# Layer 1's first neighbour stage as seven half-size products in place of eight

## The chip, the cores and the metric

The kernel runs on one core of a Trainium2 chip. The metric is the device time of one execution in microseconds (us); a shorter time is better. Before the change the median of three runs is 2171.74 us (2170.61 to 2173.77). The core has a matrix engine (TensorE, PE in the profile, with its weight loads as PEld), three engines for elementwise work (VectorE or DVE, ScalarE or ACT, GpSimd or POOL), and a queue engine for loads (SyncE or SP). Matrix products are written to PSUM, everything else lies in SBUF.

## The reference, cut to what matters

The program is a network of two layers on a graph of 625 nodes with 1024 features each. Layer 0 (edge attention, linear attention, a small quantised feed-forward) and most of layer 1 (linear attention, attention, a mixture of eight experts) are not touched. What is touched is the graph part of layer 1:

```python
def _sage_layer(h, edge_src, edge_dst, deg_inv, W_self, W_neigh, b):
    msg = h[edge_src]
    agg = jax.ops.segment_sum(msg, edge_dst, num_segments=h.shape[0])
    mean = agg * deg_inv[:, None]
    return h @ W_self + mean @ W_neigh + b
h = jax.nn.relu(_sage_layer(x, edge_src, edge_dst, deg_inv, W_self0, W_neigh0, b0))
out = _sage_layer(h, edge_src, edge_dst, deg_inv, W_self1, W_neigh1, b1)
```

Here `x` is the normalised input. The first of the two layers, with its relu, is "the first neighbour stage": a product of the pair (x, mean), 625 x 2048, with the stacked weights (W_self0 above W_neigh0), 2048 x 1024. All of it is fp32. The residual `x + out + attention` also gets two bias rows, `b1` of this part and `bo` of the attention.

## The kernel before, in words

Features lie on the partitions: `xnT1`, `meanT` and `hT` hold 1024 features as 8 blocks (`KC`) of 128 partitions, with 626 columns, one for each node and one of padding, taken as two halves of 313 (`HN`). A matmul takes a 128x128 block of weights and 313 columns. `feat` (it calls `group`, L137, whose line all these matmuls carry) makes one block of 128 output features: for each half of the columns a sum over 16 pairs, 8 of them with `xnT1` and 8 with `meanT`. The first neighbour stage calls it for the 8 output blocks `m`; ScalarE adds the bias `b0_t` and applies the relu in one instruction (L1274). Weights come as `Half` tiles: two loads of 1 MB for 512 of the 1024 output columns, from the pool `wpool` with six buffers of 1 MB.

The order of the instructions on the engines around the change is written out by hand: what stands first in the program stands first in its engine's queue. `do(prep, pe, after, after2)` is a small pipeline: each call first runs the pending `after` steps of earlier calls, then issues its own matmuls, and keeps its own `after` for the next call. PSUM tiles of two banks (`ps2`) exist three times, so the fourth user waits for what reads the first.

Four stages follow each other here. First comes the linear attention's query loop: for each `m`, `lin1.query(m + 1)` (16 matmuls into `pq`, then two ScalarE activations and L340 on VectorE for `qf`) and `lin1.answer(m)` (two matmuls into `pd`, two into `po`; then on VectorE L356 on `pd`, a reciprocal L357, and L358, which multiplies `po` into `oT`). In the first five rounds `rows_of(1, m)` is called as well: L1215 normalises 512 columns of x, and ScalarE and L1196 split the result into a high and a low part (`xnh`, `xnl`). Second comes the mean stage, `pa`: for each `k`, 20 matmuls with the adjacency counts `CTr`, and then two multiplications by the inverse degree on VectorE (L1253), which write `meanT`. The last `answer` lies inside it, at `k == 1`. Third comes the first neighbour stage, `ph`. Fourth comes `neighbours(0)`, with 40 matmuls into `pz` that read `hT`, and then `last_of`, which reads x (`px`).

At `m == 0` and `m == 4` of the first neighbour stage SP also loads a bias row (`b1`, then `L1_bo`) into `b_t`, and GpSimd adds it to the five tiles of x (L1266, ten instructions). GpSimd's queue reaches them as soon as the row has landed, whatever TensorE is at. Behind them stand two small loads for `g_t`, and stores of zeros to `rows_d` and `y_d`, whose source tile `zero` is set by L1313.

Of the kernel before, what the change touches and what calls it, by code (L numbers as in the profile page):

```python
# [8 lines left out]
FP = mybir.dt.float32  # L9
# [4 lines left out]
AF = mybir.ActivationFunctionType  # L14
ALU = mybir.AluOpType
# [5 lines left out]
NT = 5  # L21
P = 125
NP = 626
HN = 313
# [5 lines left out]
D = 1024  # L30
KC = D // 128
# [11 lines left out]
def gps_kernel(tc: tile.TileContext, w: dict, out: bass.AP):  # L43

    again = attempt(tc, w, out, False)
    with tc.If(again > 0):
        attempt(tc, w, out, True)  # L50
# [3 lines left out]
def attempt(ctx: ExitStack, tc: tile.TileContext, w: dict, out: bass.AP, shifted: bool):  # L54

    nc = tc.nc
# [10 lines left out]
    def ps2(name):  # L67
        return psums[-1][0].tile([128, 2, 512], FP, tag="ps2", name=name, bufs=3)
# [44 lines left out]
    class Half:  # L113


        def __init__(self, pool, src, c, tag="w", padded=None, now=True):
            v = src.rearrange("(k p) n -> p k n", p=128)
            self.parts = []

            def load():  # L120
                i = len(self.parts)
                t = pool.tile([128, 4, 512], FP, tag=tag, name="w", padded_shape=padded)
                self.parts.append(t)
                return nc.sync.dma_start(out=t, in_=v[:, 4 * i:4 * i + 4, c * 512:(c + 1) * 512])

            self.load = lambda: behind(load(), latest["pe"])
            if now:
                load()
                load()
# [4 lines left out]
    def group(dst, pairs):  # L134

        for i, (lhsT, rhs) in enumerate(pairs):
            made = nc.tensor.matmul(dst, lhsT=lhsT, rhs=rhs, start=(i == 0), stop=(i == len(pairs) - 1))  # L137
        latest["pe"] = made.ins.name
# [3 lines left out]
    def behind(ins, name):  # L142

        tc.add_manual_dep(ins.ins, name, mybir.DependencyInfo(mybir.DependencyClass.Sync,
                                                              mybir.DependencyReason.DATA), reason="pace")
        return ins

    def feat(name, pairs):

        p = ps2(name)  # L150
        for h in range(2):
            group(p[:, h, :HN], [(a, b[:, h * HN:(h + 1) * HN]) for a, b in pairs])
        return p[:, :, :HN]

    def halves(ap):
        return ap.rearrange("p (h n) -> p h n", h=2)
# [32 lines left out]
    class Stream:  # L189
# [7 lines left out]
        def __call__(self, prep=None, pe=None, after=None, after2=None):  # L197
            if prep is not None:
                prep()
            for steps in self.open:  # L200
                if steps:
                    steps.pop(0)()
            self.open = [steps for steps in self.open if steps]
            if pe is not None:
                pe()
            self.open.append([f for f in (after, after2) if f is not None])
# [15 lines left out]
    do = Stream()  # L222
    hold = {}

    def mid(shape, name):
        return midp.tile(shape, FP, tag="mid", name=name)

    def bigT(name):
        return big.tile([128, KC, NP], FP, tag="big", name=name, padded_shape=[128, KC, 640])
# [133 lines left out]
    with ExitStack() as st0:  # L363
# [8 lines left out]
        with ExitStack() as edges:  # L372
# [22 lines left out]
            def load_edges():  # L395
                for dst, name in ((si, "src"), (di, "dst")):
# [16 lines left out]
                                      in_=none.unsqueeze(1).to_broadcast([128, 28, 440]))  # L413
# [398 lines left out]
            for m in range(KC):  # L812
# [11 lines left out]
                if m < 3:  # L824
# [3 lines left out]
                                             in_=w[("w_gate", "w_up", "w_down")[m]]  # L828
# [9 lines left out]
            kept = mid([P, 2, 512], "kept")  # L838
# [18 lines left out]
        x = xpool.tile([P, NT, D], FP, name="x")  # L857
# [245 lines left out]
        for p in range(NT + 2):  # L1103
# [15 lines left out]
            if p == 0:  # L1119
                xnT1 = bigT("xnT1")  # L1120
# [40 lines left out]
    few = ctx.enter_context(tc.tile_pool(name="few", bufs=1, side="right", reuse_waits="tile"))  # L1161
# [1 line left out]
    sage = mixed_up.enter_context(tc.tile_pool(name="sage", bufs=1, reuse_waits="tile"))  # L1163
    dinv = sage.tile([128, NP], FP, name="dinv")
    dinvT = few.tile([P, NT], FP, name="dinvT")
    b0_t = mix.tile([128, KC], FP, tag="bq", name="b0_t", bufs=2)
    nc.gpsimd.dma_start(out=b0_t, in_=w["b0"])

    def degrees():
# [40 lines left out]
    def rows_of(c, t):  # L1210
        if c:
            xh = mix.tile([P, 512], FP, tag=("kb", "ke")[t % 2], name="xh", bufs=1)
        else:
            xh = mix.tile([128, NP], FP, tag="qf", name="xh", bufs=2)[:P, 0:512]
        nc.vector.tensor_scalar(xh, x[:, t, c * 512:(c + 1) * 512], mv1[:, t, 0:1],  # L1215
                                rs1[:, t:t + 1], op0=ALU.subtract, op1=ALU.mult)
        split(xh, xnh[c][0][:, t, :], xnh[c][1][:, t, :])
# [12 lines left out]
    for m in range(KC - 1):  # L1230
        lin1.query(m + 1)
        lin1.answer(m, oT)
        if m < NT:
            rows_of(1, m)
    meanT = []
    for k in range(KC):
        if k == 1:
            lin1.answer(KC - 1, oT)
        if k % 4 == 0:
            meanT.append(mid([128, 4, NP], "meanT"))  # L1240

        def pe():
            p = hold["pa"] = ps2("pa")

            for h in range(2):
                group(p[:, h, 0:HN + 1], [(xp[:, s, k % 4 * 128:k % 4 * 128 + 128],
                                           CTr[:, s, h * (HN - 1):h * (HN - 1) + HN + 1])
                                          for xp in xnh[k // 4][:1 if shifted else 2] for s in range(NT)])

        def after(k=k):  # L1250
            m = meanT[k // 4][:, k % 4, :]
            for h in range(2):
                nc.vector.tensor_tensor(m[:, h * HN:(h + 1) * HN], hold["pa"][:, h, h:h + HN],  # L1253
                                        dinv[:, h * HN:(h + 1) * HN], op=ALU.mult)

        do(None, pe, after)
    hT = []
    for m in range(KC):
        if m % 4 == 0:
            ws, wn = Half(wpool, w["W_self0"], m // 4), Half(wpool, w["W_neigh0"], m // 4)  # L1260
            hT.append(mid([128, 4, NP], "hT"))

            b_t = mix.tile([128, D], FP, tag="kv", name="b_t", bufs=2)
            nc.sync.dma_start(out=b_t, in_=w[("b1", "L1_bo")[m // 4]].to_broadcast([128, D]))
            for t in range(NT):
                nc.gpsimd.tensor_tensor(x[:, t, :], x[:, t, :], b_t[:P], op=ALU.add)  # L1266
        a = m % 4

        def pe():
            hold["ph"] = feat("ph", [(ws(k, a * 128, 128), xnT1[:, k, :]) for k in range(KC)]  # L1270
                              + [(wn(k, a * 128, 128), meanT[k // 4][:, k % 4, :]) for k in range(KC)])

        def after(m=m):
            nc.scalar.activation(halves(hT[m // 4][:, m % 4, :]), hold["ph"], AF.Relu, bias=b0_t[:, m:m + 1])  # L1274

        do(None, pe, after)
    z, ws, wo = [], [], []

    def neighbours(c):

        zc = big.tile([P, 2, NT, 512], NUM, tag="big", name="z")
        z.append(zc)
        wn1 = Half(wpool, w["W_neigh1"], c)
        ws.append(Half(wpool, w["W_self1"], c))
        wo.append(Half(wpool, w["L1_Wo"], c))
        for t in range(NT):
            def pe():
                hold["pz"] = ps1("pz")
                group(hold["pz"][:P], [(hT[k // 4][:, k % 4, nodes(t)], wn1(k)) for k in range(KC)])

            def after(t=t):
                split(hold["pz"][:P], zc[:, 0, t, :], zc[:, 1, t, :])

            do(None, pe, after)

    neighbours(0)
    mixed_up.close()


    rows_d = dram.tile([N + 1, D], FP, name="rows_d")  # L1300
# [15 lines left out]
    for b in range(NB_MIN, NB):  # L1316
        nc.gpsimd.dma_start(out=y_d[b * 128:(b + 1) * 128, :].rearrange("p (a n) -> p a n", a=4),
                            in_=zero.unsqueeze(1).to_broadcast([128, 4, 256]))
# [61 lines left out]
    wq = [Half(wpool, w["Wq"], c) for c in range(2)]  # L1380
# [247 lines left out]
    hT = bigT("hT")  # L1628
# [82 lines left out]
    def small(name):  # L1711
        return pool.tile([P, NT], FP, name=name)
# [10 lines left out]
    for i in range(2):  # L1723
        m = small(f"best{i}")
# [4 lines left out]
        first = small(f"first{i}")  # L1729
# [6 lines left out]
    e2, p1 = small("e2"), small("p1")  # L1736
# [7 lines left out]
    both = pool.tile([P, NT, NE], FP, name="both")  # L1744
# [146 lines left out]
    with tc.manual_schedule(engines={mybir.EngineType.PE, mybir.EngineType.DVE, mybir.EngineType.Pool}):  # L1891
        def fetch(t):

            pair = []
            for i, (tag, n) in enumerate((("xg", 2), ("yb", 2))):
                yg = pool.tile([128, D], FP, tag=tag, name="yg", bufs=n)
                nc.gpsimd.indirect_dma_start(out=yg, out_offset=None, in_=y_d[:, :],
                                             in_offset=bass.IndirectOffsetOnAxis(ap=place[:, i, t:t + 1], axis=0))
                pair.append(yg)
            return pair  # L1900
# [14 lines left out]
        pairs = [fetch(0), fetch(1)]  # L1915
# [97 lines left out]
```

## Time and profile before

| what | value |
|---|---|
| median of three runs | 2171.74 us (2170.61 to 2173.77) |
| the profiled execution, its time | 2175.02 us |
| its span, first to last instruction | 2173.3 us |
| mean granted TensorE clock | 0.987 |
| TensorE, VectorE, ScalarE, GpSimd busy | 96%, 33%, 9%, 15% of the span |
| query loop and last query, first `pq` to first `pa` | 666.05 to 757.08 us |
| mean stage, first `pa` to first `ph` | 757.08 to 786.80 us |
| first neighbour stage, first `ph` to first `pz` | 786.80 to 921.66 us |
| `pz`, first to first `px` | 921.66 to 955.99 us |
| GpSimd's additions to x (L1266) | five at 725.02 to 737.60, five at 858.01 to 869.58 us |
| memory traffic | 301.63 MB, mean 139 GB/s |

All times of stages are microseconds from the start of the span of the one profiled execution, which is 3.3 us above the median. An fp32 matmul of the program is two records of the profile. The duration of a matmul record is that of a pipelined instruction; what it costs is read from the distance between starts. Busy time of an engine says nothing of waits: the waits stand in brackets in the timeline.

### The profile page before, as it was taken

How to read it: one execution, taken by the hardware profiler on the slowest of the kernel's cores; microseconds unless marked ns; L12 is line 12 of the kernel's file. 1: busy time of each engine (PE TensorE's matmuls, PEld its weight loads, DVE VectorE, ACT ScalarE, POOL GpSimd, SP SyncE). 2: the span in 40 equal slices, each digit the busy share in tenths (PEclk: the TensorE clock that was granted, in tenths of full speed). 3: DMA queues.
4: the chain of work that ended last, by engine and by line, in shares of the span. 5: the costliest groups of instructions: out<-in, count | busy, mean ns of one | idle time of the engine just before them, and what ended most of it. 6: DMA issues, size and time to landing. Idle time of an engine off the chain costs nothing. (4 is left out here: it accounts for less than half of the span.)

```text
span 2173.3 us, 17398 instructions
## 1 busy us (share of the span) xinstructions
PE 2096.6 (96%) x6934; PEld 1202.3 (55%) x6934; DVE 712.4 (33%) x1214; ACT 194.4 (9%) x355; POOL 327.6 (15%) x329
## 2 busy tenths in 40 slices
PE   8999999499999999999999999999999999999998
PEld 6665674265446677744456776467644444444443
DVE  5786486566443720000032334212111111111012
ACT  2000110011211100000000111100000000000000
POOL 1777767200000202010000000100000000000011
PEclk9999999699999999999999999999999999999999
DMA  6632352440302202131203101122299978997832
GB/s 221 209 112 83 115 198 81 113 139 1 122 4 78 87 1 87 44 140 40 77 0 126 59 0 40 34 92 97 79 366 344 328 275 324 329 328 265 294 134 86
DMA packets 147925, 301.63 MB, mean 139 GB/s; under 512 B 12411, under 2 KB 25602, under 8 KB 147830
## 3 DMA queue, kind: packets, MB, share of 16 engines
q1 hardware_dynamic: 127548, 252.54, 33.0%
q0 software_dynamic: 15296, 37.61, 5.5%
q10 hardware_dynamic: 4986, 10.22, 1.5%
q8 instruction: 58, 0.95, 0.2%
q14 instruction: 37, 0.30, 0.0%
HBM read 277.49 MB, written 22.84 MB: 138 GB/s over the span
## 5 line engine op out<-in xcount | busy, mean ns | idle before, releaser
L137 PE MATMUL pu<-w,xgT 128*128 128x512 f32 x768 | 333.9, 593 | 1.9 <-DVE xgT L1307 1.9
L137 PEld LDWEIGHTS pu<-w,xgT 128*128 128x128 f32 x768 | 144.0, 190 | 174.8 <-issue 171.7
L137 PE MATMUL pyb<-w,hb 128*128 128x512 f32 x384 | 174.3, 599 | 2.5 <-ACT yb L105 2.1
L137 PE MATMUL pk<-w,xnT 128*125 128x512 f32 x320 | 140.8, 593 | 2.2 <-ACT xnT L1065 2.2
L137 PE MATMUL pv<-w,xnT 128*125 128x512 f32 x320 | 140.8, 593 | 0.9 <-DVE x L947 0.9
L137 PE MATMUL pq<-xnT,w 128*128 128x313 f32 x512 | 138.2, 429 | 0.8 <-DVE v L293 0.8
L137 PE MATMUL p<-tT,w 128*128 128x313 f32 x512 | 136.3, 428 | 0.4 <-DVE tT L1307 0.4
L137 PEld LDWEIGHTS pyb<-w,hb 128*128 128x128 f32 x384 | 69.9, 189 | 90.9 <-issue 74.8
L1847 DVE TENSOR_TENSOR su<-pu,su 128x512 f32<-128x512 f32 x24 | 16.6, 691 | 314.6 <-ACT su L1846 314.6
L137 PEld LDWEIGHTS pq<-xnT,w 128*128 128x128 f32 x512 | 97.5, 191 | 39.6 <-DVE v L293 1.6
L137 PEld LDWEIGHTS p<-tT,w 128*128 128x128 f32 x512 | 96.8, 190 | 37.9 <-issue 1.2
L766 PE MATMUL px<-w,oT 128*125 128x512 f32 x160 | 72.8, 612 | 32.2 <-DMA table<-es,at 28.0
L137 PEld LDWEIGHTS pk<-w,xnT 128*125 128x125 f32 x320 | 59.2, 188 | 74.1 <-issue 71.2
L137 PEld LDWEIGHTS pv<-w,xnT 128*125 128x125 f32 x320 | 59.4, 188 | 73.5 <-issue 71.3
L641 POOL DMA_INDIRECT table<-es,at x79 | 85.5, 1083 | 59.9 <-issue 24.6
L1830 POOL DMA_INDIRECT xg<-rows_d,slots x12 | 11.3, 943 | 524.8 <-PE pxg L1837 449.0
L621 POOL DMA_INDIRECT ga<-xl_d,si x79 | 79.8, 1010 | 30.1 <-issue 21.6
L621 POOL DMA_INDIRECT gb<-xr_d,di x79 | 79.6, 1007 | 24.1 <-issue 22.0
L1196 DVE TENSOR_TENSOR z<-pz,z 125x512 fp32r<-125x512 f32 x10 | 6.9, 692 | 196.8 <-ACT z L1194 196.8
L137 PE MATMUL px<-w,hT 128*125 128x512 f32 x160 | 70.3, 592 | 0.0
L137 PE MATMUL px<-w,oT 128*125 128x512 f32 x160 | 70.3, 592 | 0.0
L766 PEld LDWEIGHTS px<-w,oT 128*125 128x125 f32 x160 | 30.4, 193 | 72.0 <-issue 36.9
(362 smaller groups left out, 2531.6 us busy)
## 6 DMA issues: line engine op xcount, KB each, us to landing
w<-in_eW_dram SPq DMA_DIRECT2D x144, 1024.0 KB
w<-in_L_Wk_dram SPq DMA_DIRECT2D x8, 1024.0 KB
w<-in_L_Wv_dram SPq DMA_DIRECT2D x8, 1024.0 KB
w<-in_L_Wq_dram SPq DMA_DIRECT2D x8, 1024.0 KB
w<-in_L_Wo_dram SPq DMA_DIRECT2D x8, 1024.0 KB
w<-in_W_self_dram SPq DMA_DIRECT2D x8, 1024.0 KB
w<-in_W_neigh_dram SPq DMA_DIRECT2D x8, 1024.0 KB
w<-in_sW_dram SPq DMA_DIRECT2D x8, 1024.0 KB
```

What stands on the lines that cost most here:

```text
L137: made = nc.tensor.matmul(dst, lhsT=lhsT, rhs=rhs, start=(i == 0), stop=(i == len(pairs) - 1))
L621: got = nc.gpsimd.indirect_dma_start(out=ab[g][side][0:p, j, :], out_offset=None, in_=src[:, :], in_offset=bass.IndirectOffsetOnAxis(ap=ix ...
L641: put = nc.gpsimd.indirect_dma_start(out=table[:, :], out_offset=bass.IndirectOffsetOnAxis(ap=at[0:p, lo + j:lo + j + 1], axis=0), in_=es[ ...
L766: made = nc.tensor.matmul(hold["px", t][:P, c, :], lhsT=oT[:, k, nodes(t)], rhs=wo[c](k), start=(k == 0), stop=(k == KC - 1 and keep is no ...
L1196: nc.vector.tensor_tensor(low, src, high.bitcast(FP), op=ALU.subtract)
L1830: nc.gpsimd.indirect_dma_start(out=xg, out_offset=None, in_=rows_d[:, :], in_offset=bass.IndirectOffsetOnAxis(ap=slots[:, b:b + 1], axis=0))
L1847: nc.vector.tensor_tensor(su, pu[:, 0, :], su, op=ALU.mult)
```

## The change

The first neighbour stage is written as a product of 2x2 blocks by Strassen's scheme in a form with seven products. The four blocks of the right side are x and the mean by the two halves of the columns: A11 and the tail from `xnT1`, A12 and A22 from `meanT`. The blocks of the weights are W_self0 and W_neigh0 by the two halves of the output columns, and these are worked through in two quarters of 256 columns (`Quarter`), so that a quarter's four weight blocks are 1 MB each. Each quarter makes seven products of 16 matmuls (2 output blocks x 8 `k`), with the same 128x128 by 313 columns.

VectorE makes what the scheme adds. Four sums of right-hand blocks, S1 to S4 (two instructions each, 128x1252), of which S3 overwrites the tail of `xnT1`; four mixes of weight blocks for each quarter (`third`, `second`, `first`, `fourth`, 128x2048 each), the first two of the first quarter placed in the mean stage at `k == 5` and `k == 6`; and the sums of the products out of PSUM (`add`, `done`). ScalarE copies the first product of a quarter out of PSUM, and applies the relu with the bias to 128x313 at a time.

The order of the products is: A11, A12, S2, S3, A22, S1, S4. The second quarter's weights are loaded into the buffers that the first quarter's products leave. `b0_t` moves to the pool `few`. The two bias rows are loaded by GpSimd's queue into a new pool `seven`, are added to each other once, and the sum is added to the five tiles of x, all by VectorE in the second quarter. GpSimd's ten additions are gone. The pools `mix` and `sage` are closed before the stage in place of after `neighbours(0)`.

```diff
-    b0_t = mix.tile([128, KC], FP, tag="bq", name="b0_t", bufs=2)
+    b0_t = few.tile([128, KC], FP, name="b0_t")
...
+    class Quarter:
+        def __init__(self, i):
+            lo = 256 * i
...
+            self.source = {"12": ("W_self0", 512 + lo), "11": ("W_self0", lo),
+                           "22": ("W_neigh0", 512 + lo), "21": ("W_neigh0", lo)}
+        def room(self, name):
+            self.tiles[name] = wpool.tile([128, KC, 256], FP, tag="w", name="wq" + name)
+        def load(self, *names):
...
+                nc.sync.dma_start(out=self.tiles[name],
+                                  in_=w[src].rearrange("(k p) n -> p k n", p=128)[:, :, lo:lo + 256])
+        def mix(self, dst, a, b, op):
+            nc.vector.tensor_tensor(self.tiles[dst], self.tiles[a], self.tiles[b], op=op)
+        def third(self):
+            self.mix("12", "22", "12", ALU.subtract)
+        def second(self):
+            self.mix("2", "12", "11", ALU.add)
+        def first(self):
+            self.mix("11", "22", "2", ALU.subtract)
+        def fourth(self):
+            self.mix("21", "21", "2", ALU.subtract)
+
+    quarters = [Quarter(0), Quarter(1)]
+    quarters[0].room("2")
+    quarters[0].load("12", "21", "11", "22")
     for k in range(KC):
         if k == 1:
             lin1.answer(KC - 1, oT)
+        if k == 5:
+            quarters[0].third()
+        if k == 6:
+            quarters[0].second()
...
-    hT = []
-    for m in range(KC):
-        if m % 4 == 0:
-            ws, wn = Half(wpool, w["W_self0"], m // 4), Half(wpool, w["W_neigh0"], m // 4)
-            hT.append(mid([128, 4, NP], "hT"))
-
-            b_t = mix.tile([128, D], FP, tag="kv", name="b_t", bufs=2)
-            nc.sync.dma_start(out=b_t, in_=w[("b1", "L1_bo")[m // 4]].to_broadcast([128, D]))
-            for t in range(NT):
-                nc.gpsimd.tensor_tensor(x[:, t, :], x[:, t, :], b_t[:P], op=ALU.add)
-        a = m % 4
-        def pe():
-            hold["ph"] = feat("ph", [(ws(k, a * 128, 128), xnT1[:, k, :]) for k in range(KC)]
-                              + [(wn(k, a * 128, 128), meanT[k // 4][:, k % 4, :]) for k in range(KC)])
-        def after(m=m):
-            nc.scalar.activation(halves(hT[m // 4][:, m % 4, :]), hold["ph"], AF.Relu, bias=b0_t[:, m:m + 1])
-        do(None, pe, after)
+    do()
+    mixed_up.close()
+    seven = ExitStack()
+    spool = seven.enter_context(tc.tile_pool(name="seven", bufs=1, reuse_waits="tile"))
+    hT = [mid([128, 4, NP], "hT") for i in range(2)]
+    b_t = [spool.tile([128, D], FP, name=f"b_t{i}") for i in range(2)]
+    for b, name in zip(b_t, ("b1", "L1_bo")):
+        nc.gpsimd.dma_start(out=b, in_=w[name].to_broadcast([128, D]))
+    S1, S2, S4 = (spool.tile([128, KC, HN], FP, name=f"S{i}") for i in (1, 2, 4))
+    head, tail = slice(0, HN), slice(HN, NP)
+    S3 = xnT1[:, :, tail]
...
+    def sum1(k, mean):
+        nc.vector.tensor_tensor(S1[:, k, :], xnT1[:, k, tail], mean[:, :, tail], op=ALU.add)
+    def sum2(k, mean):
+        nc.vector.tensor_tensor(S2[:, k, :], S1[:, k, :], xnT1[:, k, head], op=ALU.subtract)
+    def sum3(k, mean):
+        nc.vector.tensor_tensor(S3[:, k, :], xnT1[:, k, head], xnT1[:, k, tail], op=ALU.subtract)
+    def sum4(k, mean):
+        nc.vector.tensor_tensor(S4[:, k, :], mean[:, :, head], S2[:, k, :], op=ALU.subtract)
...
+        def product(name, right, after):
+            def pe():
+                kept[0] = ps2("pw")
+                for a in range(2):
+                    wt = q.tiles[name]
+                    group(kept[0][:, a, :HN], [(wt[:, k, a * 128:(a + 1) * 128], right[k]) for k in range(KC)])
+            return lambda: do(None, pe, lambda: after(kept[0][:, :, :HN]))
...
+        return [product("11", A11, lambda p: nc.scalar.activation(u, p, AF.Copy)),
+                product("21", A12, lambda p: done(0, head, p, u)),
+                product("2", S2k, lambda p: add(u, p, u)),
+                product("12", S3k, lambda p: add(u3, p, u)),
+                product("21", A22, lambda p: done(0, tail, p, u3)),
+                product("11", S1k, both),
+                product("22", S4k, lambda p: done(1, head, p, u))]
+
+    now, then = quarters
+    then.load("12")
+    p1, p2, p6, p7, p4, p5, p3 = quarter(now)
+    four(sum1)
+    four(sum2)
+    p1()
+    p2()
+    now.first()
+    four(sum3)
+    p6()
+    now.fourth()
+    four(sum4)
+    then.load("11")
+    p7()
+    then.load("22")
+    p4()
+    then.load("21")
+    p5()
+    then.third()
+    p3()
+    then.room("2")
+    p1, p2, p6, p7, p4, p5, p3 = quarter(then)
+    p1()
+    then.second()
+    p2()
+    then.first()
+    p6()
+    then.fourth()
+    nc.vector.tensor_tensor(b_t[0], b_t[0], b_t[1], op=ALU.add)
+    p7()
+    for t in range(2):
+        nc.vector.tensor_tensor(x[:, t, :], x[:, t, :], b_t[0][:P], op=ALU.add)
+    p4()
+    for t in range(2, NT):
+        nc.vector.tensor_tensor(x[:, t, :], x[:, t, :], b_t[0][:P], op=ALU.add)
+    p5()
+    p3()
...
     neighbours(0)
-    mixed_up.close()
+    seven.close()
```

More of the change, by code (lines that the diff above doesn't have):

```diff
@@ L1235, in attempt @@
     meanT = []
+    class Quarter:
+        def __init__(self, i):
+            lo = 256 * i
+            self.i = i
+            self.tiles = {}
+            self.source = {"12": ("W_self0", 512 + lo), "11": ("W_self0", lo),
[3 more added lines that the diff above has]
+        def load(self, *names):
+            for name in names:
+                self.room(name)
+                src, lo = self.source[name]
+                nc.sync.dma_start(out=self.tiles[name],
[13 more added lines that the diff above has]
+    quarters[0].load("12", "21", "11", "22")
     for k in range(KC):
@@ new lines, in attempt, with four @@
+    S3 = xnT1[:, :, tail]
+    def four(f):
+        for j in range(2):
+            f(slice(4 * j, 4 * j + 4), meanT[j])
+    def sum1(k, mean):
[6 more added lines that the diff above has]
+        nc.vector.tensor_tensor(S4[:, k, :], mean[:, :, head], S2[:, k, :], op=ALU.subtract)
@@ new lines, in attempt, with quarter, pairs, add @@
+    A11 = [xnT1[:, k, head] for k in range(KC)]
+    A12, A22 = ([meanT[k // 4][:, k % 4, h] for k in range(KC)] for h in (head, tail))
+    S1k, S2k, S3k, S4k = ([S[:, k, :] for k in range(KC)] for S in (S1, S2, S3, S4))
+    def quarter(q):
+        i = q.i
+        kept = {}
+        u = spool.tile([128, 2, HN], FP, tag="u", name="u", bufs=2)
+        u3 = spool.tile([128, 2, HN], FP, tag="u", name="u3", bufs=2)
+        def pairs(name, a, right):
+            wt = q.tiles[name]
+            return [(wt[:, k, a * 128:(a + 1) * 128], right[k]) for k in range(KC)]
+        def product(name, right, after):
+            def pe():
+                kept[0] = ps2("pw")
+                for a in range(2):
+                    wt = q.tiles[name]
+                    group(kept[0][:, a, :HN], [(wt[:, k, a * 128:(a + 1) * 128], right[k]) for k in range(KC)])
+            return lambda: do(None, pe, lambda: after(kept[0][:, :, :HN]))
+        def add(dst, a, b):
+            nc.vector.tensor_tensor(dst, a, b, op=ALU.add)
+        def done(c, h, a, b):
+            dst = hT[c][:, 2 * i:2 * i + 2, h]
+            add(dst, a, b)
+            for a in range(2):
+                m = 4 * c + 2 * i + a
+                nc.scalar.activation(dst[:, a, :], dst[:, a, :], AF.Relu, bias=b0_t[:, m:m + 1])
+        def both(p):
+            done(1, tail, p, u3)
+            add(u, p, u)
+        return [product("11", A11, lambda p: nc.scalar.activation(u, p, AF.Copy)),
[5 more added lines that the diff above has]
+                product("22", S4k, lambda p: done(1, head, p, u))]
```

## The prediction

> **What bounds the kernel now.** I read the page's first part first, to see which engine the span belongs to, then its groups for the changed stage.
>
> ```profile
> PE 2096.6 (96%) x6934; PEld 1202.3 (55%) x6934; DVE 712.4 (33%) x1214; ACT 194.4 (9%) x355; POOL 327.6 (15%) x329
> ```
>
> TensorE is busy for 96% of the span, so whatever it no longer executes, or no longer waits for, comes off the end unless something else becomes late. Next, the groups of instructions by tile for `ph`, the stage's PSUM tile, and the busy time by stretch (from:to, length, then busy us and instructions of TensorE, its weight loads, VectorE, ScalarE and GpSimd, the granted clock, the DMA share, GB/s):
>
> ```profile
> L137 PE MATMUL ph<-xnT,w x256: 424/427/427, 786.8 to 917.2; 128*128 128x313 f32 x128
> L137 PE MATMUL ph<-meanT,w x256: 424/426/428, 791.0 to 921.4; 128*128 128x313 f32 x128
> 786.80:921.66 134.86, 134.86 (x515) 96.94 (x513) 0.87 (x2) 5.48 (x7) 12.60 (x7) 1.00 0.14 49
> ```
>
> The program's 256 matmuls stand as 512 records, two each. The 427 ns is the latency of a pipelined record, not its cost: `pz`, the next stage, starts at 921.66, so the stage lasts 134.86 us, 527 ns a matmul. TensorE has no gap in it, the clock is 1.00, VectorE works 0.87 us, and the DMA share is 0.14. So the stage costs its matmuls and nothing else.
>
> The diff also takes L1266, ten additions on GpSimd, away. Who runs beside them is in the timeline from 718 to 748 us (start, duration, engine, line; in brackets the idle time before and what ended it):
>
> ```profile
> 721.45 0.54 DVE L1215 TENSOR_SCALAR xh<-x,mv,rs 125x512 f32<-125x512 f32 x1
> 722.69 0.69 DVE L1196 TENSOR_TENSOR xnl<-xh,xnh 125x512 fp32r<-125x512 f32 x1 [0.70 <-ACT xnh L1194]
> 725.02 9.86 POOL L1266 TENSOR_TENSOR x<-x,b_t 125x1024 f32<-125x1024 f32 x4 [130.55 <-DMA b_t<-in_b_dram]
> ...
> 731.26 1.40 DVE L340 SCALAR_TENSOR_TENSOR qf<-qe,qf 128x626 f32<-128x626 f32 x1 [2.15 <-ACT qf L339]
> ...
> 732.59 2.57 DVE L1215 TENSOR_SCALAR xh<-x,mv,rs 125x512 f32<-125x512 f32 x1
> ...
> 735.24 2.36 POOL L1266 TENSOR_TENSOR x<-x,b_t 125x1024 f32<-125x1024 f32 x1 [0.36 <-DVE xh L1215]
> 735.86 2.29 DVE L1196 TENSOR_TENSOR xnl<-xh,xnh 125x512 fp32r<-125x512 f32 x1 [0.70 <-ACT xnh L1194]
> ...
> 743.94 2.38 PE L137 MATMUL po<-qf,kv 128*128 128x313 f32 x4 [2.66 <-DVE oT L358]
> ```
>
> Beside the first five GpSimd additions, three VectorE instructions of the attention loop take 1.40, 2.57 and 2.29 us where they take 0.81, 0.54 and 0.69 an iteration earlier: 4.22 us late. VectorE's reciprocal chain behind them ends late with `oT`, and TensorE's `po` waits for it 2.66 us. The stretch after it shows a second price:
>
> ```profile
> 701.40:711.94 10.54, 10.54 (x42) 7.59 (x41) 7.55 (x6) 2.09 (x4) 0.00 (x0) 1.00 0.39 132
> 743.94:747.20 3.26, 3.26 (x7) 2.15 (x8) 1.60 (x2) 1.46 (x2) 0.00 (x0) 0.52 0.00 0
> ```
>
> After the wait the granted clock is 0.52 for 3.26 us. The period from one `pd` to the next is 10.54 us (718.98, 729.52, 740.06); the next `pd` comes at 755.21, not 750.60. The collision therefore costs **4.61 us** on the path.
>
> [...] the three above are held, while the reciprocal (4.07 us) and `oT` (one input in PSUM, 0.81 us) at 724 to 729, beside the same additions, are not. [...]
>
> **The change part by part.**
>
> *Matmuls.* Seven products of 16 matmuls for each of two quarters make 224 in place of 256, same shape (weights 128x128, 313 columns, fp32). 32 x 527 ns = **−16.86 us**. Each product lasts 16 x 527 ns = 8.43 us, the new stage 118.0 us.
>
> *GpSimd additions gone.* **−4.61 us**: L340 to L1196 go back to their usual durations, `oT` is written about 4.2 us earlier, at 739.7, and `po` is due at 741.1. The second five, 858.01 to 869.58, ran beside an idle VectorE and are worth nothing. The second wait of this kind, `po` at 763.75 (2.30 us, its chain starts at the last query's end), stays. The half clock behind it (0.54 over 764.8 to 768.2, about 1.6 us) may fall otherwise when the first is gone: ±1.6 us.
>
> *Weight mixes, `third` and `second`,* are put into VectorE's queue inside the mean stage, in front of the mean multiplications of k = 4 and 5; TensorE's PSUM tiles wait behind those. Their weights sit in the buffers that the fifth and sixth loads of before had (issued 753.30, when the last query frees them; both MB are in by 762, DMA at 393 GB/s). In before's times: k = 3's multiplication ends at 776.24, third until 778.5, k = 4 until 779.5 (due 778.29), second until 781.8, k = 5 until 782.7, k = 6 on time at 784.1. TensorE first needs k = 4's tile for k = 7, at about 783.9. Cost 0 under 4.4 us of cover; even mixes of double length would give some 0.4 us.
>
> *Sums and mixes in the stage,* times from its start, all on VectorE in program order, products numbered as they run. S1 and S2 (four of 1.46 us behind the last mean multiplication) are ready at 7.1; product three needs S2 at 16.9. `first` waits for product one, is done at 10.9, S3 at 13.8, needed at 25.3. `fourth` stands behind product two's PSUM addition: 20.2, needed at 33.7; S4 23.1, needed at 50.6. In the second quarter `second` waits behind product seven's addition: 62.3, needed at 75.9. The smallest margin is 9.8 us. In total: eight sums 11.7, six mixes 13.7, fourteen PSUM additions (0.81, L358's row) 11.3, six additions of biases and x 7.3 (1.22 each): 44 us of VectorE in 118. A product's PSUM tile is wanted again three products on, 16.9 us later, and needs one 0.81 us addition. ScalarE has 2 copies of 0.78 and 16 relus of about 0.5 (0.496 for the 128x256 row): 9.6 us. Cost 0. What if a sum were late: 1 us for 1 us, plus some 1.7 of half clock.
>
> *Weight loads.* Eight of 1 MB as before. SP now waits before each of the second quarter's: issued at about 25, 34 and 42 us, after products three, four and five. Their first readers are product one at 59, `third`, which VectorE reaches at about 43, and product two at 67; two such loads together took under 9 us (753.30 to 762). The next stages' loads queue behind these on SP. W_neigh1's halves find buffers at 59 and 93 us, long before `pz`. The last three, of W_self1 and L1_Wo, go out from the stage's end to 2.5 us after it, where before they went from 6.1 us ahead of it to 0.3 behind; they are read 34 us later, after `pz`. Cost 0.
>
> *GpSimd's queue.* The two bias loads come from SP to it; behind them stand only the g, zero and y_d stores, which waited for the stage's last relu (922.70) and now wait for VectorE alone. b0's load moves to another pool without a new wait there. The biases' sum and x's five additions stand in VectorE's queue behind products two, three and four of the second quarter, 1.22 to 3.7 us ahead of PSUM additions with 16.9 us of room; x is read at `px`, after `pz`. Cost 0.
>
> *The stage's end.* The last product's addition and first relu, 0.81 + 0.5 us and some 0.4 of hand-over, stand before `pz`'s seventh matmul, 6 x 0.86 = 5.2 us after the end. Cost 0.
>
> Sum: −16.86 − 4.61 = **−21.5 us**. The profiled execution took 2175.02 us with a span of 2173.3; the span goes to 2151.8, that execution to 2153.5. The median of the runs shown is 3.3 us below the profiled one: 2171.74 − 21.5 = **2150.3 us**.
>
> **The rivals.** *The stall stays (B).* If `po` waits for VectorE for another reason, only the matmuls are won: −16.9, 2154.9 us. For it: the chain is tight, a reciprocal takes 4.07 us of a 10.54 us period. Against: five earlier iterations do the same work with no wait. *A product waits (C).* A late mix or load, or hand-overs at fourteen product starts, gives back 5 to 12 us: 2155 to 2162 us. For it: VectorE goes from 0.87 to 44 us in this stage and works in order, so one wait at its head delays all. Against: margins of 3.5 us and more everywhere. *Slower (D).* VectorE's traffic slows the matmuls themselves. The place is the 224 matmuls; the gain is gone at (134.86 + 4.61)/224 = 623 ns each, and at 680 ns the time is 2184.6 us. Against: in the query loop VectorE is busy 72% of the period and 16 matmuls still take 8.43 us, the same 527 ns. *The change doesn't do what it says:* the matmuls would have to be limited by weight loads; those are busy 97 of 134.86 us, and hidden; and they fall by an eighth too.
>
> **How the numbers follow.** A (−21.5) 0.76, B 0.11, C 0.09, D or no change 0.04. A's own range is ±3 us, from the clock's ±1.6 and runs that spread from 2170.61 to 2173.77. The range 2146.5 to 2157 takes in A, B and the near end of C. A measurement of this kernel tells 0.2% (4.3 us) from no change: faster by more 0.95 (A, B and nearly all of C), within 0.02, slower 0.03.
>
> **What would show it.** Right: `pw` in 448 records over 118 us with clock 1.00 and no wait on VectorE; L340, L1215 and L1196 at their usual durations throughout; one wait of `po` for `oT` instead of two; the `pd`s six times 10.54 us apart. Wrong: a wait of `pw` for a wq or S tile, the mean stage longer than its 29.7 us (757.1 to 786.8) by over 1.6, a slow VectorE row beside a store from GpSimd, or `pz` and `px` waiting for a load.

## The result, and the profile after

The changed kernel takes 2147.43 us (median of 4 runs, 2145.6 to 2149.7) beside 2172.76 us (4 runs, 2170.61 to 2175.14) for the kernel before: a ratio of 0.9884, 95% interval 0.9867 to 0.9901. A second measurement, made later and with more runs, gave 2151.01 us (6 runs) beside 2170.88 us (11 runs), ratio 0.9907 (0.9887 to 0.9928). The forecast of 21.5 us less is a ratio of 0.9901, which lies inside the second interval and just at the upper end of the first. The kernel before has medians from 2170.88 to 2201.64 us in the four measurements made here, so times are only compared within one measurement.

The profiled execution took 2148.84 us with a span of 2147.1 us, 26.2 us less span than before. The page's first part:

```profile
PE 2072.1 (97%) x6870; PEld 1184.0 (55%) x6870; DVE 754.5 (35%) x1250; ACT 197.6 (9%) x365; POOL 303.5 (14%) x321
```

TensorE lost 64 records, 32 matmuls, and 24.5 us of busy time; VectorE gained 42 us of work, GpSimd lost 24. The groups of instructions by tile, here for `pw`, the new stage's PSUM tile (duration in ns as least, median and most; first and last start):

```profile
L137 PE MATMUL pw<-S,wq x192: 424/426/429, 794.2 to 895.3; 128*128 128x313 f32 x192
L137 PE MATMUL pw<-xnT,wq x128: 424/427/427, 777.4 to 869.9; 128*128 128x313 f32 x128
L137 PE MATMUL pw<-meanT,wq x128: 424/426/428, 785.8 to 878.4; 128*128 128x313 f32 x128
```

That is 448 records of the old duration, and the list of TensorE's waits has none of a `pw`. Busy time by stretch (from:to and length; busy us and instructions of TensorE, weight loads, VectorE, ScalarE, GpSimd; granted clock, DMA share, GB/s), for the query loop, the mean stage, the neighbour stage, and the time behind the wait of `po` that is left:

```profile
662.82:749.24 86.42, 86.42 (x353) 63.54 (x352) 47.21 (x39) 15.81 (x25) 0.00 (x0) 1.00 0.13 43
749.24:777.39 28.15, 25.84 (x170) 24.83 (x169) 22.02 (x23) 0.00 (x0) 2.14 (x4) 1.00 0.21 71
777.39:895.53 118.14, 118.14 (x451) 84.84 (x449) 42.38 (x35) 8.41 (x16) 7.67 (x13) 1.00 0.30 103
755.90:759.40 3.50, 3.50 (x21) 3.20 (x22) 3.46 (x4) 0.00 (x0) 1.60 (x3) 1.00 0.17 41
```

TensorE fills the query loop and the neighbour stage without a gap, at full clock. The first two rows' lengths were 91.03 and 29.72 us before. In the last row, the clock stayed at 1.00 after 2.31 us of waiting, where the kernel before had 0.54 at this place. Side by side:

| stretch | before, us | after, us | difference |
|---|---|---|---|
| ahead of the query loop (first `pq`) | 666.05 | 662.82 | −3.23 |
| query loop, to the first `pa` | 91.03 | 86.42 | −4.61 |
| mean stage, to the first product | 29.72 | 28.15 | −1.57 |
| first neighbour stage, to `pz` | 134.86 | 118.14 | −16.72 |
| rest of the span | 1251.64 | 1251.57 | −0.07 |
| sum | | | −26.20 |

Now VectorE's rows in the query loop, from the timeline (start, duration, engine, line; in brackets the idle time before it and what ended that):

```profile
728.03 0.81 DVE L340 SCALAR_TENSOR_TENSOR qf<-qe,qf 128x626 f32<-128x626 f32 x1 [2.15 <-ACT qf L339]
728.76 0.54 DVE L1215 TENSOR_SCALAR xh<-x,mv,rs 125x512 f32<-125x512 f32 x1
730.00 0.69 DVE L1196 TENSOR_TENSOR xnl<-xh,xnh 125x512 fp32r<-125x512 f32 x1 [0.69 <-ACT xnh L1194]
```

The three rows that were 4.22 us late have their usual durations. The `pd`s start at 684.14, 694.67, 705.21, 715.75, 726.29, 736.83 and 747.37: six times 10.54 us. The list of TensorE's waits keeps one for `oT`:

```profile
PE po L137 <- DVE oT L358: 2.3, 1, 2.3
```

The new work on VectorE, from the timeline of the mean stage and the start of the neighbour stage:

```profile
766.75 2.28 DVE L1258 TENSOR_TENSOR wq<-wq,wq 128x2048 f32<-128x2048 f32 x1
...
778.38 2.82 DVE L1319 TENSOR_TENSOR S<-xnT,meanT 128x1252 f32<-128x1252 f32 x2
781.12 2.83 DVE L1322 TENSOR_TENSOR S<-S,xnT 128x1252 f32<-128x1252 f32 x2
...
794.25 5.97 PE L137 MATMUL pw<-S,wq 128*128 128x313 f32 x22
```

A mix takes 2.28 us. A 1252-element sum takes 1.45 to 1.46 us, and two in a row 2.82 to 2.83, since each starts a little before the one ahead of it ends. S2 (L1322) is ready at 783.95, 6.6 us into the stage, and its product starts at 794.25, exactly where the two products ahead of it end.

The first row of the table belongs to code that the change doesn't touch. It is uneven by itself. One group ahead of the query loop, in the timeline of before and then of after (both 40 matmuls of `pg`, preceded by a wait of the same 1.08 us):

```profile
465.85 7.10 PE L137 MATMUL pg<-xl,pT 125*125 125x65 f32 x40 [1.08 <-ACT xnT L1065]
```

```profile
464.21 4.58 PE L137 MATMUL pg<-xl,pT 125*125 125x65 f32 x40 [1.08 <-ACT xnT L1065]
```

The same work took 2.52 us longer in the one execution, at a mean granted clock of 0.62 instead of 1.00 over that stretch. In the thirteen profiles told of here, all of kernels that are identical up to the query loop, its first `pq` stands between 662.82 and 693.82 us; on one chip alone, four of them lie between 682.36 and 693.82. Against a spread of 11.5 us on one chip, 3.23 us can't be put down to the change. What is left in the stages that the change touches is −4.61 − 1.57 − 16.72 = −22.9 us.

### The profile page after: what moved, and what is told of

It reads as the page before. It is cut to its first block, busy times and chain, and to the rows that moved or that the text cites. A ratio compares the mean times of both kernels' runs of the same rounds, so it can differ in the third digit from the quotient of the medians.

```text
span 2147.1 us, 17319 instructions
## 1 busy us (share of the span) xinstructions
PE 2072.1 (97%) x6870; PEld 1184.0 (55%) x6870; DVE 754.5 (35%) x1250; ACT 197.6 (9%) x365; POOL 303.5 (14%) x321
## 5 line engine op out<-in xcount | busy, mean ns | idle before, releaser
L137 PE MATMUL pX<-w,aT 128*125 128x512 f32 x160 | 69.3, 592 | 0.0
```

## The experiments

The theory: 527 ns for each of 32 matmuls, and the end of a meeting between GpSimd's additions and three VectorE instructions in the query loop. The rivals: the stall of `po` has another cause and stays; the additions cost time wherever they stand; the margins of the new VectorE work are not real, and the stage is only just fed. The last experiments ask what GpSimd would do to the new work.

**The additions alone.** The kernel before, with its eight products; GpSimd's additions go to VectorE, at m == 6 of the `ph` stage.

```diff
+            b_rows.append(b_t)
+        if m == 6:
+            nc.vector.tensor_tensor(b_rows[0], b_rows[0], b_rows[1], op=ALU.add)
             for t in range(NT):
-                nc.gpsimd.tensor_tensor(x[:, t, :], x[:, t, :], b_t[:P], op=ALU.add)
+                nc.vector.tensor_tensor(x[:, t, :], x[:, t, :], b_rows[0][:P], op=ALU.add)
```

> Kernel before, eight products, but the two bias rows are summed and added to x by VectorE at m = 6 of the first neighbour stage; GpSimd adds nothing. Theory [...]: the distance from the sixth to the seventh pd is 10.5 us, not 15.2, po waits for oT once, the stage stays 134.9 us; 2166.6 to 2168.2 us (the lower end if the half clock behind the remaining wait goes too). Rival (the wait had another cause): 15.2 us stays, 2172.8 us. Rival (all that the change gained beyond 16.9 us is here): 2164.3 us.

Measured: 2190.12 us (8 runs) beside 2195.7 (28 runs), ratio 0.9977 (0.9957 to 0.9998), which is −5.0 us (−9.4 to −0.4). The stretches of the query loop and the mean stage:

```profile
684.22:770.64 86.42, 86.42 (x354) 63.53 (x352) 47.22 (x39) 15.82 (x25) 0.00 (x0) 1.00 0.17 58
770.64:798.79 28.15, 25.85 (x171) 24.83 (x169) 17.81 (x21) 0.00 (x0) 0.00 (x0) 1.00 0.13 46
```

Without one Strassen product, both have the lengths that they have in the changed kernel. The kernel before, profiled once more as a control on the same chip, has 91.35 and 29.69 us there:

> The kernel before, unchanged, for a second profile. Shows how far the start of the query loop (666.05 us before, 662.82 after) and the half clock behind the second wait of po differ from one execution to the next. If the half clock (mean stage 29.7 us, with it gone 28.15) is a consequence of the first wait, it stands here again, and in the run with the products alone, and in neither of the other two; if it depends on the moment, it is spread over all four.

Its one time was 2195.72 us; its waits for `oT` were 2.98 and 2.31 us, with a clock of 0.57 behind the first and 0.66 behind the second. So the collision of the old profile was no single accident.

**The same additions, later.** The kernel before, with all ten additions still on GpSimd, but the first row's load held until the `ph` stage.

```diff
+        if m in (1, 4):
             b_t = mix.tile([128, D], FP, tag="kv", name="b_t", bufs=2)
-            nc.sync.dma_start(out=b_t, in_=w[("b1", "L1_bo")[m // 4]].to_broadcast([128, D]))
+            put = nc.sync.dma_start(out=b_t, in_=w[("b1", "L1_bo")[m // 4]].to_broadcast([128, D]))
+            if m == 1:
+                behind(put, latest["pe"])
```

> Kernel before, eight products, all ten additions still on GpSimd, but the first row's load waits for the first output block's matmuls, so that they run while VectorE is idle. Theory (the additions cost only where they meet VectorE): as with VectorE's additions, 10.5 us between the pds, 2166.6 to 2168.2 us. Rival (the additions cost wherever they run, or only their absence gains): 2172.8 us.

Measured: 2192.98 us (20 runs), ratio 0.9982 (0.9966 to 0.9997), −4.0 us (−7.5 to −0.7). From the timeline:

```profile
759.03 0.81 DVE L340 SCALAR_TENSOR_TENSOR qf<-qe,qf 128x626 f32<-128x626 f32 x1 [2.15 <-ACT qf L339]
829.82 11.57 POOL L1269 TENSOR_TENSOR x<-x,b_t 125x1024 f32<-125x1024 f32 x5 [207.58 <-DMA b_t<-in_b_dram]
```

The additions still take 11.57 us, but 50 us after the query loop, in a stage where VectorE has next to nothing to do (0.87 us of 134.86 in the first profile of before). The loop lasts 86.42 us and the mean stage 28.15, beside 91.35 and 29.69 in the control. The meeting costs the time, not the additions and not the engine that makes them.

**The products alone.** The changed kernel, with the first bias row loaded early and added to x by GpSimd as before; the second row stays with VectorE.

```diff
-    quarters[0].load("12", "21", "11", "22")
+    quarters[0].load("12", "21", "11")
+    b_early = mix.tile([128, D], FP, tag="kv", name="b_early", bufs=2)
+    nc.sync.dma_start(out=b_early, in_=w["b1"].to_broadcast([128, D]))
+    for t in range(NT):
+        nc.gpsimd.tensor_tensor(x[:, t, :], x[:, t, :], b_early[:P], op=ALU.add)
+    quarters[0].load("22")
...
-    nc.vector.tensor_tensor(b_t[0], b_t[0], b_t[1], op=ALU.add)
```

> Kernel after with seven products, but GpSimd adds the first bias row to x as early as in the kernel before (the second row stays with VectorE in the stage). Theory: three VectorE rows of the query loop are held again, po waits 2.7 us, sixth to seventh pd 15.2 us, the stage 118.0 to 118.2 us; 16.9 us below before, 2155.9 us. Rival (what vanished was due to the moved loads or pools): 10.5 us and about 2147.5 us.

Measured: 2182.37 us (5 runs), ratio 0.9936 (0.9907 to 0.9965), −14.1 us (−20.4 to −7.7). The collision is back, and dearer. Timeline:

```profile
742.44 9.86 POOL L1278 TENSOR_TENSOR x<-x,b_early 125x1024 f32<-125x1024 f32 x4 [131.66 <-DMA b_early<-in_b_dram]
...
747.58 2.51 DVE L340 SCALAR_TENSOR_TENSOR qf<-qe,qf 128x626 f32<-128x626 f32 x1 [2.14 <-ACT qf L339]
...
750.01 2.57 DVE L1215 TENSOR_SCALAR xh<-x,mv,rs 125x512 f32<-125x512 f32 x1
...
753.28 2.28 DVE L1196 TENSOR_TENSOR xnl<-xh,xnh 125x512 fp32r<-125x512 f32 x1 [0.70 <-ACT xnh L1194]
...
761.36 2.45 PE L137 MATMUL po<-qf,kv 128*128 128x313 f32 x4 [3.69 <-DVE oT L358]
```

L340 asked 5.14 us after the additions began, where it was 6.24 in the kernel before, and lost 1.70 us instead of 0.59. The loop is 93.30 us long, 6.88 over the free one; part of that is that the half clock behind the wait lasted 6.83 us here. The neighbour stage is 118.14 us all the same (803.80 to 921.94), so the two parts of the change add up. And the mean stage is 28.14 us, with clock 1.00 behind the second wait, although the first wait was there (clock 0.50 behind it). So the first wait alone doesn't bring the half clock at the second.

**Are the margins real?** The changed kernel, with ten needless sums of 1252 elements put on VectorE ahead of S1.

```diff
     p1, p2, p6, p7, p4, p5, p3 = quarter(now)
+    for i in range(10):
+        nc.vector.tensor_tensor(S4[:, 4 * (i % 2):4 * (i % 2) + 4, :], xnT1[:, 0:4, head], xnT1[:, 0:4, tail], op=ALU.add)
     four(sum1)
```

> Kernel after, with ten needless VectorE sums of 1.41 us ahead of S1 (written to S4, which is overwritten later). They put S2's readiness from about 6.6 us after the stage's start to 20.7, with its product due at 16.9. Theory (VectorE's 42 us are hidden by margins, the smallest here): TensorE waits 3.8 to 4.2 us once, for S2, and may run at half clock for some 3.4 us behind it (1.7 us); stage 118.1 us up to 122 to 124. Rival (the prologue is not the smallest cover, the sums hide elsewhere): 118.1 us.

Measured, in one execution: 2177.24 us; the stage is 120.55 us long, +2.4. Timeline:

```profile
804.30 13.82 DVE L1379 TENSOR_TENSOR S<-xnT 128x1252 f32<-128x1252 f32 x10
...
820.78 2.83 DVE L1322 TENSOR_TENSOR S<-S,xnT 128x1252 f32<-128x1252 f32 x2
822.38 2.88 PE L137 MATMUL pw<-S,wq 128*128 128x313 f32 x10 [2.18 <-DVE S L1322]
```

Of 13.82 us, all but 2.2 disappeared. The stage's third product did wait, so it is VectorE's lead that feeds it; that lead is 11.6 us, 1.8 more than reckoned, mostly because the product starts when the first of S2's two instructions is done (820.78 + 1.45 = 822.23). The wait came out smaller than expected for the same reason. Half clock behind a wait was seen in the kernel before, 0.54 from 764.80 to 768.20; here the clock stayed at 1.00 behind it, from 822.38 to 825.80.

**GpSimd beside the mixes.** The changed kernel, with x's additions as ten GpSimd instructions as soon as the rows are in, beside the mean stage; VectorE's six are gone.

```diff
         nc.gpsimd.dma_start(out=b, in_=w[name].to_broadcast([128, D]))
+    for i in range(2):
+        for t in range(NT):
+            nc.gpsimd.tensor_tensor(x[:, t, :], x[:, t, :], b_t[i][:P], op=ALU.add)
...
```

> Kernel after, with ten additions to x on GpSimd in place of VectorE's six, free to run as soon as the rows land, so beside the mean stage and the stage's first sums. Theory [...]: the mean multiplications (one input in PSUM) keep 0.47 us, the two weight mixes of 2.28 us and the sums of 1.41 us that meet an addition take up to 2.35 us longer each; cover of 4.4 us in the mean stage and 9.8 us before S2 absorbs most: 0 to 2 us on TensorE, no slow row from 787 us on. Rival (VectorE is held for every addition): 10 to 23 us of VectorE late and a wait of several us on TensorE.

Measured, in one execution: 2192.09 us, a single time that says little by itself. The mean stage is 40.56 us long, +12.4; the neighbour stage is unchanged at 118.14. Timeline:

```profile
788.88 23.39 POOL L1312 TENSOR_TENSOR x<-x,b_t 125x1024 f32<-125x1024 f32 x10
...
797.58 16.84 DVE L1258 TENSOR_TENSOR wq<-wq,wq 128x2048 f32<-128x2048 f32 x1
...
815.35 1.65 PE L137 MATMUL pa<-CT,xnh 125*128 125x314 f32 x5 [9.88 <-DVE meanT L1296]
```

A mix of 2.28 us took 16.84: VectorE asked at 797.58, during GpSimd's fourth addition, and went on only when the tenth had ended at 812.27. The expectation of at most one addition's length, 2.35 us, for each mix was wrong. The mean multiplications, which have one input in PSUM, were not held: beside the first additions four of them took 1.68 us at 793.08 and two took 0.88 at 796.78, as elsewhere (0.86 to 0.88 for two). The pair queued behind the mix only started at 814.34, and the next mix, at 815.12, took 2.28. TensorE waited 9.88 us, and its groups of five `pa` matmuls took 1.65 us behind that in place of 0.89.

**Is it the operation, or its length?** In the query loop L340 did get in between two additions: it took 1.40 us in the kernel before, 1.73 in its control and 2.51 with the products alone, where it takes 0.81 undisturbed. It is a `scalar_tensor_tensor`, and shorter than the mix of 2.28 us. Two kernels change `third` of the last one: to that operation, and to four pieces of 512 elements.

```diff
-            self.mix("12", "22", "12", ALU.subtract)
+            t = self.tiles
+            nc.vector.scalar_tensor_tensor(t["12"], t["22"], 1.0, t["12"], op0=ALU.mult, op1=ALU.subtract)
```

```diff
-            self.mix("12", "22", "12", ALU.subtract)
+            t = self.tiles
+            for h in range(4):
+                ks = slice(2 * h, 2 * h + 2)
+                nc.vector.tensor_tensor(t["12"][:, ks, :], t["22"][:, ks, :], t["12"][:, ks, :], op=ALU.subtract)
```

> The kernel with ten GpSimd additions beside the mean stage[...]. Here that mix is a scalar_tensor_tensor (times 1.0, then subtract)[...]. If the operation decides: the mix takes under 5 us and TensorE waits 0 to 1 us. [...] about 16.8 us again and a wait near 10 us.

> The same kernel with the first weight mix cut into four tensor_tensor of 512 elements. If length decides (a short instruction fits between two additions, as L340 of 626 elements did): each takes up to 2.9 us, the mix some 5 to 10 us. If not: the first of the four waits for the last addition, and the mean multiplications behind it are late by as much as before, a wait near 10 us on TensorE.

Measured, one execution each: 2163.6 and 2163.75 us. The mix in the first and in the second timeline:

```profile
769.89 16.48 DVE L1262 SCALAR_TENSOR_TENSOR wq<-wq,wq 128x2048 f32<-128x2048 f32 x1
```

```profile
769.17 17.05 DVE L1264 TENSOR_TENSOR wq<-wq,wq 128x512 f32<-128x512 f32 x4
```

Neither helps: 16.48 and 17.05 us are near the 16.84 of the plain mix. GpSimd's additions ran until 784.2 and 783.9, and TensorE waited 9.5 and 10.1 us. In the query loop, in all three profiles in which the two met, L340 asked during the third addition and got its turn when that one ended, though the fourth was queued. (L1215's turn ahead of the fifth is of another kind: that addition overwrites the tile of x that L1215 reads, and waits for it, 0.36 us in the kernel before.) Why VectorE got one turn there and none here stays open.

**The wait that is left.** The changed kernel, with the last query's answer put one mean step later.

```diff
-        if k == 1:
+        if k == 2:
             lin1.answer(KC - 1, oT)
```

> Kernel after, with the last answer of the linear attention at k = 2 of the mean stage in place of k = 1. Theory: the one wait of po for oT that is left (2.3 us, in every profile so far) is covered by one more k of pa (2.9 us); mean stage 28.15 us down to 25.9 to 26.4, the rest unchanged, 1.8 to 2.3 us below after. Rival: the wait moves to pd, whose PSUM tile the same VectorE instruction frees, or to pa; 28.15 us stays, 0.

Measured: 2180.37 us (6 runs) beside 2201.64 (11 runs), ratio 0.9889 (0.9859 to 0.992). The mean stage:

```profile
780.24:806.52 26.28, 25.81 (x170) 24.89 (x169) 22.01 (x23) 0.00 (x0) 2.14 (x4) 1.00 0.22 78
```

It is 1.87 us shorter than 28.15; a wait of 0.5 us takes the place of the 2.31. To see whether times show it, this kernel and the changed one were measured together on one more chip:

> The kernel after, unchanged, beside the next one on one chip. Ratio to before 0.988 to 0.990 by the theory (23.0 us of 2172 from matmuls, collision and clock: 0.9894). Mean stage 28.15 us, or 29.7 if the half clock behind the second wait depends on the moment alone.

> The kernel after with the last answer at k = 2. Mean stage 26.28 us again, 1.9 us below the kernel after in the profile; by the times 0.9875 to 0.9895 of before, which this measurement may not tell from the kernel after.

The changed kernel: 2151.01 us, ratio 0.9907 (0.9887 to 0.9928), the second measurement told of above. With the later answer: 2147.75 us (5 runs), 0.9886 (0.9867 to 0.9905), mean stage 26.31 us. It beats the kernel before; that it beats the changed one is shown by the stage's length in two profiles, while the times don't separate the two.

## Why the prediction was right

**Matmuls.** −16.86 us was forecast, −16.72 measured, and the stage was 118.13 or 118.14 us long in all seven further profiles with seven products, other than the one with the needless sums told of above. The 0.14 us is what is left of rival C: fourteen product starts cost nearly nothing. Rival D falls with it: VectorE's 42.4 us in the stage left the matmuls at 527 ns.

**GpSimd additions gone.** −4.61 us was forecast and measured, to the hundredth. The exactness is that of one trace: the sum was read off the `pd`s' period of the same execution, and the loop did become undisturbed. In other executions the collision cost 4.93 us (the kernel before, again) and 6.88 (with the products alone). The three late rows add up to 4.22 us, but only 2.66 of that reached TensorE as a wait; most of the rest of the 4.61 is the half clock behind it, 0.52 for 3.26 us, or about 1.6 us. Rival B is refuted by the two kernels that take the meeting away in different ways: with the additions on VectorE, and with the additions on GpSimd but later, one wait goes and the loop is 86.42 us. What holds the three rows was not shown; only that they are late beside the additions and on time without them.

**The half clock behind the second wait.** The text gave ±1.6 us and took 0; it came out as −1.57, and that was luck: the traces tie it to the execution, not to the change. The wait of 2.3 us before the last `po` stands in eleven of the profiles. Half clock follows it in three: both of the kernel before (0.54, 0.66) and one variant of the changed kernel, the one with the `scalar_tensor_tensor` mix, whose own edits all take effect later (0.53, against 1.00 at the same place in its sister with four pieces). In the other eight, one with the collision among them, the clock is 1.00.

The traces show what sets them apart. In each of the thirteen, all changes of the granted clock lie a whole number of steps of 3.413 us from each other, and this grid of steps lies differently against the program in each execution. These are the step that holds most of the wait and the step after it, first in the kernel with the `scalar_tensor_tensor` mix, then in the one with four pieces:

```profile
753.89:757.31 3.42, 1.33 (x6) 0.68 (x5) 3.32 (x2) 0.00 (x0) 0.00 (x0) 1.00 0.32 125
757.31:760.72 3.41, 3.19 (x8) 2.45 (x9) 3.38 (x5) 0.00 (x0) 0.44 (x1) 0.50 0.00 0
```

```profile
754.56:757.97 3.41, 1.46 (x7) 0.81 (x5) 3.31 (x2) 0.00 (x0) 0.00 (x0) 1.00 0.31 120
757.97:761.38 3.41, 3.06 (x18) 2.76 (x19) 3.38 (x5) 0.00 (x0) 1.42 (x2) 1.00 0.05 10
```

TensorE was busy for 0.39 of the step in the first and for 0.43 in the second. Over the eleven profiles, the step with the most of the wait was busy for a share of 0.33, 0.33 and 0.39 where half clock followed, and for 0.43 to 0.56 where it did not. The other waits in these stages agree: those of 2.66, 2.98 and 3.69 us left a step busy for 0.22, 0.13 and 0.23, and half clock followed; the one of 2.18 us for S2 left 0.47, and none did. So by these profiles what sets them apart is how much of a wait fell into one step, and for 2.3 us that depends on where the grid lies. No experiment moved a wait to test this, and it is no rule for the whole program: ahead of the query loop, in the kernel before, half clock also followed a step that was busy for 0.68 (2.33 of the 3.41 us from 464.15 to 467.56).

**Edits costed at nothing.** The mixes in the mean stage, the sums, weight loads, bias loads and stores all cost nothing: the list of waits names none of them, and the mean stage is 28.15 us long with the mixes and, in the kernel with the additions alone, without them. The author's estimates of VectorE's durations held: 2.28 us for 2.29, and 1.45 to 1.46 for 1.46. The kernel before has no `tensor_tensor` of these lengths, but three groups of shorter ones (behind the bar: busy us, mean ns of one):

```profile
L1196 DVE TENSOR_TENSOR xnh<-xh,xnh 125x512 fp32r<-125x512 f32 x5 | 3.5, 692 | 5.0 <-ACT xnh L1194 5.0
L947 DVE TENSOR_TENSOR x<-px,x 125x1024 f32<-125x1024 f32 x5 | 6.1, 1224 | 2.9 <-PE px L942 2.9
L568 DVE TENSOR_TENSOR wd<-wd,rw 128x1024 f32<-128x1024 f32 x1 | 1.2, 1214 | 0.0
```

Straight lines from 0.692 us at 512 elements through 1.214 and 1.224 at 1024 lead to an estimate of 1.45 to 1.46 us at 1252 and 2.26 to 2.29 at 2048. VectorE's total was 42.4 us for 44, ScalarE's 8.4 for 9.6. The margin before S2 was not only argued: it absorbed 11.6 us of extra work.

**The sum.** −21.5 us forecast, −22.9 found by the profiles in the stages concerned, of which −21.3 without the half clock, −25.3 by the first measurement and −19.9 by the second. The profiles' further −3.2 is no missed mechanism: it stands ahead of the query loop, in code that is the same, and changes from execution to execution. In us, the intervals are −28.9 to −21.5 and −24.5 to −15.6. Both hold −22.9; −21.3 lies in the second and just outside the first. The two measurements differ by more than the half clock is worth, so the times can't say how often it falls.

**What was not seen.** The forecast treats VectorE's cover for the mixes in the mean stage, 4.4 us, as safe, to within 0.4 us, for "even mixes of double length". It held with no GpSimd additions there (mean stage 28.15 us). With ten additions beside it the same cover was overrun by 9.9 us.

## What to carry to other kernels

Where TensorE was the bound and its stage had no gaps, a matmul saved was worth its period in that stage (16.72 us for 32, which is nearly the 527 ns of the period and not the 427 of the record), with the engine that prepares the operands running ahead; test that lead by giving it needless work, as the 13.82 us of sums did here. Five GpSimd additions, 12.58 us from first to last, sat on the critical path of a stage that they have nothing to do with, and cost it 4.61 us, by holding VectorE's instructions (two with two SBUF inputs, 1.40 and 2.29 us for 0.81 and 0.69, and a `tensor_scalar`, 2.57 for 0.54). Before moving such work to another engine, look for a stage where VectorE is idle: here moving it in time brought the query loop to 86.42 us, as moving it to VectorE did.

## What the runs showed of the hardware

- In the mean stage, back-to-back GpSimd additions held a VectorE instruction with two SBUF inputs until the last of them ended: 16.84 us for a 2.28 us `tensor_tensor`, 16.48 as `scalar_tensor_tensor`, 17.05 in four pieces. The author had reckoned with a wait for one addition at most (2.35 us), and it was the rest of one and six more. In the query loop L340 did get a turn between two additions, in three profiles of three (1.40, 1.73 and 2.51 us for its 0.81).
- The granted clock changed on a grid of 3.413 us, in each of the thirteen profiles. In the changed stages, half clock came after a step in which TensorE was busy for 0.39 or less (waits of 2.66, 2.98, 3.69 and 9.88 us, and three of 2.3), and not where waits left every step at 0.43 or more (eight of 2.3 us and one of 2.18).
- The start of the query loop, behind identical code, varied over 31 us between executions and chips, more than the whole change is worth, and by 11.5 us on one chip.
